# A scan kernel's outer product by TensorE for one block in eight, evictions moved to ScalarE, and the last output moved into the next stage

## The chip, the cores and the metric

One NeuronCore of a Trainium2 chip runs the whole program. The metric is the device time of one execution in microseconds (us). The profile names the engines PE (TensorE matmuls), PEld (TensorE weight loads), DVE (VectorE), ACT (ScalarE), POOL (GpSimd) and SP (SyncE, which here only issues DMAs).

## What is computed

The input has 4 images of 32 x 32 positions and 256 channels; an image is 1024 tokens. Layer 0 is a convolution block with a selective scan: layer norm, a projection to 512 channels, a depthwise 3 x 3 convolution, GELU, and then for each of 64 states a recurrence over the tokens. Layer 1 is an attention that is linear in the tokens, and a mixture of 16 experts of which each token takes two. Cut to what matters:

```python
proj = x @ w_x;  dt_raw, Bm, Cm = split(proj)           # 16, 64 and 64 columns
dt = softplus(dt_raw @ w_dt + dt_bias);  A = -exp(A_log)
def step(h, inp):                                       # over the 1024 tokens
    dA = exp(dtt[:, :, None] * A)
    h = dA * h + (dtt * xt)[:, :, None] * Bt[:, None, :]
    return h, einsum('bdn,bn->bd', h, Ct)
y = layernorm(ys + x * D_skip) * g2 + b2
x = src + y @ w_out + b_out                             # end of layer 0
t = x as tokens
t = t + attention(ln(t));  t = t + experts(ln(t))       # layer 1
```

## The kernel before, in words

**The scan.** The work is cut into 8 units: 4 images times two halves of 512 tokens. Unit 2b is the first half of image b, unit 2b+1 the second half, which starts from the state that the first half left (`last`, line 714). A unit runs over 64 states n, and each state over 4 blocks m of 128 channels: 256 slots a unit, one scan instruction a slot. In a slot:

- `scale` (line 684, ACT): `bx`, the 512 channels of 128 tokens (block j) times B of those tokens, tokens on the partitions. Four of them make a state.
- `decay` (line 692, ACT): `da`, exp(dt * A) for one block of channels.
- `turn` (line 698, PE): four 128 x 128 transposes bring `bx` into a PSUM bank with channels on the partitions; three banks rotate.
- `scan` (line 704, DVE): the recurrence over 512 tokens. After the fourth block POOL multiplies the whole state by C (line 719), from `cb_n`, which SP fetches three states ahead.
- `add_up` (line 726, PE): four transposes add the product into the four banks of y, 9 slots later.

The order of the scan's instructions is written out by hand (`manual_schedule`, lines 803 to 864): at slot k the program issues `scale(k+8)`, `decay(k+4)`, `scan(k)`, `turn(k+3)`, `add_up(k-9)`. Each engine runs its own instructions in that order. `da` has 6 buffers and `bx` 12.

**The planner.** Work of neighbouring units is laid into the slots beside the scan (`beside`, line 753). It comes as lists of pieces (gap, engine, cost, what): `head` (layer norm and input projection, 16 long matmuls), `conv` (36 taps of the 3 x 3 convolution, line 378), `dt_bc` (dt, B and C of the next unit), `after_stats` and `after` (layer norm, output projection and residual of the unit before). Each list has a window of slots, over which its pieces fall due evenly (`CONV1 = (16, 170)` and so on, lines 793 to 798). In a slot an engine takes at most about 1.0 us of such work, by the planner's costs. The pieces that use PE share one PSUM bank, `bg`: a list takes it, runs on without regard to its due times until an eviction frees it, and then the next list may take it, in a later slot. In `conv` a group of 9 taps stands 2 slots apart, so its 36 taps cover 72 of the 256 slots. Evictions from `bg` are `put_pad` (344), `put` of conv (392), `put_dtx` (534), `put` of after (610), all on DVE.

**The last unit's output.** After the last slot, lines 866 to 871 run `after_stats`, `roots_after` and `after` for unit 7 with nothing beside them. It is written to `td` in DRAM.

**Attention.** Line 925 on: loads of the weights, loads of all four images from `td` (line 941), then the preparation of the weights (lines 945 to 1004: means taken out of the columns, and the value and output matrices multiplied), then a loop over the 4 images (line 1018): statistics (1011), `xh` (1023), transposes (120), `pqk` (1037), `pv` (1054), `pkv` (1089), `po` (1134), the gate (1161). The order of this part is set by the tile framework's own scheduler, not by hand. Routing and the experts follow from line 1210.

Of the kernel before, what the change touches and what calls it, by code (L numbers as in the profile page):

```python
# [16 lines left out]
P = 128  # L17
# [16 lines left out]
def conv_ssm_attn_moe_kernel(ctx: ExitStack, tc: tile.TileContext, a: dict, out: bass.AP):  # L34
# [92 lines left out]
    def blk(i, n=BANK):  # L127
        return slice(i * n, (i + 1) * n)
# [5 lines left out]

    with ExitStack() as l0:
# [3 lines left out]
        scanp = l0.enter_context(tc.tile_pool(name="scan", bufs=2))  # L139
        ps_y = l0.enter_context(tc.tile_pool(name="ps_y", bufs=1, space=PSUM))  # L140
        ps_w = l0.enter_context(tc.tile_pool(name="ps_w", bufs=3, space=PSUM))
# [38 lines left out]
        w_o = load_rows("L0_conv_w_out", DK, C, w0)  # L180
        b_o = load_bcast("L0_conv_b_out", C, w0)
# [33 lines left out]
        for m in range(DK):  # L215
            pad = w0.tile([P, HH + 2, WW + 2], F32, name=f"pad{m}")
            nc.gpsimd.memset(pad, 0.0)
            pads.append(pad)

        def late_weights():  # L220
# [9 lines left out]
            for m in range(DK):  # L230
                nc.vector.tensor_scalar(
                    diag_d[:, m, :], ident, dsk[:, m : m + 1], None, ALU.mult
                )

# [64 lines left out]
        def head(b, g, lo=0, hi=TPB):  # L299
# [26 lines left out]
            for i in range(lo, hi):  # L326
# [6 lines left out]
                todo.append(piece(2, "DVE", 0.42, lambda i=i: put(i), "free"))  # L333
# [9 lines left out]
            def put_pad(m):  # L343
                nc.vector.tensor_scalar(
                    pads[m][:, 1 + g * ROWS + lo * RPT : 1 + g * ROWS + hi * RPT, 1 : 1 + WW],
                    made["bg"][:, : (hi - lo) * P].rearrange("p (h w) -> p h w", w=WW),
                    b_in[:, m : m + 1], None, ALU.add,
                )

            for m in range(DK):  # L350
# [4 lines left out]
                todo.append(piece(3, "DVE", 0.75, lambda m=m: put_pad(m), "free"))  # L355
            return todo

        def conv(v):
# [30 lines left out]
            def put(m):  # L389
                if m == 0:  # L390
                    made["xg", v] = acts.tile([P, DK, BANK], F32, name="xg")
                nc.vector.tensor_scalar(
                    made["xg", v][:, m, :], made["bg"], cb[:, m : m + 1], None, ALU.add
                )
# [8 lines left out]
            for m in range(DK):  # L403
# [8 lines left out]
                todo.append(piece(3, "DVE", 0.69, lambda m=m: put(m), "free"))  # L412
# [3 lines left out]
        def dt_bc(w, needs):  # L416
# [22 lines left out]
            def put_bc():  # L439
# [3 lines left out]
                nc.sync.dma_start(out=cd, in_=t[NS:, :])  # L443
                made["bct"], made["cd", w] = t, cd
# [88 lines left out]
            def put_dtx(m):  # L533
                nc.vector.tensor_copy(  # L534
# [28 lines left out]
            for m in range(DK):  # L563
                todo.append(piece(4 if m == 0 else 1, "PE", 0.44, lambda m=m: turn_dtx(m), "take"))
                todo.append(piece(
                    2, "DVE", 0.69,
# [20 lines left out]
        def after(u, need):  # L587
# [20 lines left out]
            def put(j):  # L608
                t = pre.tile([P, DK, P], F32, name="yT")
                nc.vector.tensor_copy(t, made["bg"].rearrange("p (m t) -> p m t", m=DK))  # L610
# [19 lines left out]
            for j in range(TPB):  # L630
# [5 lines left out]
                todo.append(piece(2, "DVE", 0.69, lambda j=j: put(j), "free"))  # L636
# [7 lines left out]
            return parts + [todo]  # L644

# [37 lines left out]

        def scale(s, j):
            u, n = steps[s]
            t = scanp.tile([P, DN], F32, name="bx", bufs=12)
# [790 lines left out]
```

## Time and profile before

| | us |
|---|---|
| median of 3 runs | 3609.48 (3608.98 to 3614.11) |
| the profiled execution | 3609.15 |
| its span, first to last instruction | 3607.3 |
| before the first scan instruction | 129.7 |
| units 0 to 7 of the scan | 330.0, 341.3, 335.3, 341.3, 335.6, 337.3, 328.1, 317.9 |
| end of the last scan instruction | 2796.5 |
| first attention transpose (line 120) | 2842.1 |
| start of routing (line 1225) | 3095.1 |

The units are counted from the first scan instruction (line 712) of one to that of the next. Between the execution's time and its span lie 1.85 us. A unit's length divided by 256 is the mean time of a slot, about 1.31 us. In the groups of instructions a mean duration is longer than the distance between two starts, because neighbours overlap by some 0.1 us: what an engine can do in a unit is counted by the distance from start to start in a stretch without idle time, which the timeline shows.

### The profile page before, as it was taken

To read this page: it belongs to the slowest core of one execution; us is meant where nothing else is said; L and a number is where in the kernel's file an instruction comes from. 1 tells how busy PE (TensorE), PEld (TensorE's weight loads), DVE (VectorE), ACT (ScalarE), POOL (GpSimd) and SP (SyncE) were. 2 spreads that over 40 slices of the span, in tenths; PEclk is the share of its full clock that TensorE was granted. 3 is DMA by queue.
4 is the path that set the end of the run, shared out by engine and by line. 5 is a ranking of instruction groups with operands and counts; after the bars stand their busy time and mean duration, and the time that the engine had idled before them with its cause. 6 is when DMAs were issued, how large, how long until landed. Compare 5 with 4: busy or idle time off the path is not lost.

```text
span 3607.3 us, 60573 instructions
## 1 busy us (share of the span) xinstructions
PE 3245.6 (90%) x22292; PEld 2626.9 (73%) x22292; DVE 2981.9 (83%) x3398; ACT 2863.8 (79%) x4748; POOL 2484.2 (69%) x906
## 2 busy tenths in 40 slices
PE   8989999999998998999999989898999788599995
PEld 3678777777777777777777777777777455399985
DVE  5799999999999999999999999999999666622224
ACT  1799999999999999999999999999999244121211
POOL 0489878987897798879878987998888110033331
PEclk9999999999999999999999999999999999699997
DMA  3223222212222122222222122222121200299996
GB/s 101 64 55 76 56 64 65 61 57 58 71 69 60 62 62 61 64 63 66 60 64 64 57 59 54 55 58 57 55 60 55 73 24 12 100 381 325 319 302 236
DMA packets 355165, 334.41 MB, mean 93 GB/s; under 512 B 162081, under 2 KB 241441, under 8 KB 354866
## 3 DMA queue, kind: packets, MB, share of 16 engines
q1 hardware_dynamic: 334834, 306.21, 29.1%
q0 software_dynamic: 7104, 19.41, 1.6%
q10 hardware_dynamic: 12928, 4.89, 0.5%
q8 instruction: 177, 2.90, 0.3%
q14 instruction: 122, 1.00, 0.1%
HBM read 304.21 MB, written 25.69 MB: 91 GB/s over the span
## 4 chain that ended last, share of the span: by engine, by line
ACT 60%; PE 20%; DMA 8%; DVE 7%; issue 2%; POOL 0%; POOLq 0%; DVEq 0%; ACTq 0%; SPq 0%
ACT da L695 28%; ACT bx L687 28%; DMA yd<-yb,dst 6%; PE ps L701 4%; PE y L733 3%; PE p L1377 3%; DVE h L712 3%; PE pqk L1037 2%; PE bg L382 1%; PE pf L1389 1%; DMA xb<-xd,src 1%; PE pv L1054 1%; PE ps L382 1%; PE ps_t L120 1%; ACT L695 1%
## 5 line engine op out<-in xcount | busy, mean ns | idle before, releaser
L719 POOL TENSOR_TENSOR h<-h,cb_n 128x2048 f32<-128x2048 f32 x512 | 2143.6, 4192 | 416.7 <-DVE h L712 328.0
L701 PE MATMUL ps<-ident,bx 128*128 128x128 f32 x8192 | 1323.3, 283 | 197.8 <-DVE h L712 138.0
L687 ACT ACTIVATE bx<-dtxT,bT 128x512 f32<-128x512 f32 x2048 | 1451.5, 709 | 16.5 <-DVE dtxT L534 16.5
L695 ACT ACTIVATE da<-dt,l_conv_a_log_sb 128x512 f32<-128x512 f32 x2048 | 1452.2, 709 | 13.6 <-DVE h L712 13.3
L701 PEld LDWEIGHTS ps<-ident,bx 128*128 128x128 f32 x8192 | 937.2, 142 | 632.8 <-DVE h L712 307.9
L712 DVE TENSOR_TENSOR_SCAN h<-da,last,ps 128x512 f32<-128x512 f32 x1024 | 1231.6, 1263 | 30.3 <-ACT da L695 21.6
L733 PE MATMUL y<-ident,h 128*128 128x128 f32 x8192 | 1246.1, 275 | 5.7 <-POOL h L719 5.6
L712 DVE TENSOR_TENSOR_SCAN h<-da,ps 128x512 f32<-128x512 f32 x1024 | 1189.5, 1207 | 49.4 <-ACT da L695 32.6
L733 PEld LDWEIGHTS y<-ident,h 128*128 128x128 f32 x8192 | 974.5, 143 | 7.8 <-POOL h L719 6.7
L1383 DVE TENSOR_TENSOR hT<-s,p 128x256 f32<-128x256 f32 x148 | 62.4, 421 | 336.4 <-ACT s L1382 336.4
L1377 PE MATMUL p<-xT,w 128*128 128x128 f32 x2368 | 291.6, 277 | 0.5 <-ACT xT L1366 0.5
L1377 PEld LDWEIGHTS p<-xT,w 128*128 128x128 f32 x2368 | 285.1, 194 | 4.8 <-ACT xT L1366 0.9
L1382 ACT ACTIVATE s<-p 128x256 f32<-128x256 f32 x148 | 56.9, 384 | 275.5 <-PE p L1377 275.5
L1397 POOL DMA_INDIRECT yd<-yb,dst x74 | 73.2, 990 | 264.5 <-DMA yd<-yb,dst 185.9
L382 PE MATMUL bg<-pad,dgc 128*128 128x512 f32 x432 | 222.2, 596 | 0.0
L1346 POOL DMA_INDIRECT xb<-xd,src x74 | 72.1, 975 | 132.8 <-DVE dst L1318 108.7
L1389 PE MATMUL pf<-w,hT 128*128 128x256 f32 x592 | 153.3, 382 | 0.1
L1051 POOL TENSOR_TENSOR t_all<-t_all,bcat 128x256 f32<-128x256 f32 x32 | 23.0, 747 | 164.6 <-ACT xh L1023 159.9
L1389 PEld LDWEIGHTS pf<-w,hT 128*128 128x128 f32 x592 | 101.7, 192 | 8.2 <-DVE hT L1383 0.5
L1366 ACT COPY xT<-px 128x256 f32<-128x256 f32 x74 | 27.6, 372 | 77.5 <-PE px L1364 77.5
L382 PEld LDWEIGHTS bg<-pad,dgc 128*128 128x128 f32 x432 | 65.5, 192 | 0.0
L382 PE MATMUL ps<-pad,dgc 128*128 128x512 f32 x144 | 64.0, 605 | 0.7 <-DVE e L487 0.7
(287 smaller groups left out, 2056.5 us busy)
## 6 DMA issues: line engine op xcount, KB each, us to landing
cb_n<-cd SPq DMA_DIRECT2D x512, 256.0 KB, 3.3
w<-in_L_ffn_w_dram SPq DMA_DIRECT2D x222, 512.0 KB, 6.2
dgc<-diags SPq DMA_DIRECT2D x84, 192.0 KB, 3.1
y<-yd SPq DMA_DIRECT2D x8, 1024.0 KB, 9.6
last<-h SPq DMA_DIRECT2D x256, 2.0 KB, 2.9
xr<-in_x_dram SPq DMA_DIRECT2D x32, 128.0 KB, 3.2
td<-xr SPq DMA_DIRECT2D x32, 128.0 KB, 3.3
t_all<-td SPq DMA_DIRECT2D x4, 1024.0 KB, 10.0
```

Source lines behind the costliest of these rows:

```text
L382: nc.tensor.matmul(made["bg"].rearrange("p (h w) -> p h w", w=WW), made["dgc", m * 3 + i][:, j, :], pads[m][:, half * ROWS + i : (half + 1 ...
L687: nc.scalar.activation(t, made["dtxT", u][:, j, :], AF.Copy, scale=made["bT", u][:, j, n : n + 1])
L695: nc.scalar.activation(t, made["dt", u][:, m, :], AF.Exp, scale=A[:, m, n : n + 1])
L701: nc.tensor.transpose(t[:, blk(j, P)], made["bx", s, j][:, blk(m, P)], ident)
L712: nc.vector.tensor_tensor_scan(h[:, m, 1:], made.pop(("da", s, m)), made.pop(("dbx", s, m)), 0.0 if seg == 0 else last[b][:, n, m : m + 1] ...
L719: nc.gpsimd.tensor_tensor(h[:, :, :BANK], h[:, :, 1:], over_middle(made["c", s], DK), ALU.mult)
L733: nc.tensor.matmul(made["y", u][j][:, blk(m, P)], made["h", s][:, m, blk(j, P)], ident, is_transpose=True, start=n == 0 and m == 0, stop=n ...
L1037: nc.tensor.matmul(pqk.rearrange("p s c -> p (s c)"), xhT[:, ck, blk(i, P)], wcat[:, ck, : 2 * C], start=(ck == 0), stop=(ck == CK - 1),)
L1346: nc.gpsimd.indirect_dma_start(t, None, xd[:, :], bass.IndirectOffsetOnAxis(src[:, i : i + 1], 0))
L1377: nc.tensor.matmul(p12[:, j, s, :], on[w, i][:, ck, blk(h + j, P)], on["xT", i][:, ck, :], start=(ck == 0), stop=(ck == CK - 1),)
L1389: nc.tensor.matmul(on["pf", i], on["hT", i][:, hk, :], on["w3", i][:, hk, :], start=(hk == 0), stop=(hk == HK - 1),)
L1397: nc.gpsimd.indirect_dma_start(yd[:, :], bass.IndirectOffsetOnAxis(dst[:, i : i + 1], 0), yb, None)
```

## The change

1. **B on a diagonal.** In units 1 to 7, for even states n and the first block of tokens (j = 0), `scale` issues nothing. In its place `turn` multiplies: the block of `dtxT` (128 tokens by 128 channels) is the stationary operand and a 128 x 128 matrix with B on its diagonal the moving one, so that the product is already turned. The other three blocks stay as they were. The matrices lie in DRAM (32 for each of two units in turn): they are set to zero once, in unit 0 (slots 4 and 14), `put_bc` of each later unit writes the diagonals with a DMA of single elements, and `fetch_diagonal` loads a 64 KB matrix three states ahead, on SP's queue, into one of 3 buffers. `bx` goes from 12 buffers to 11.
2. **Evictions on ScalarE.** While an odd unit is scanned, `put_pad`, `put` of conv, `put_dtx` and `put` of after run on ACT; while an even one is, `put` of after alone. The planner's windows are new.
3. **Attention's weights** are prepared by a planner's list, `matrices`, beside unit 6, in the memory of the convolution's padded images. Their evictions run on DVE.
4. **The last half.** The output of unit 7 is no longer computed after the scan. Its sum `ysb`, `w_o` and `b_o` are kept, the residual is loaded straight from x into `t_all`, and `last_half` computes it in attention, ahead of the second image. `t_all`'s loads no longer wait for a write of unit 7. The two PSUM pools of layer 0 are opened in the other order.

```diff
+        ps_w = l0.enter_context(tc.tile_pool(name="ps_w", bufs=3, space=PSUM))
         ps_y = l0.enter_context(tc.tile_pool(name="ps_y", bufs=1, space=PSUM))
-        ps_w = l0.enter_context(tc.tile_pool(name="ps_w", bufs=3, space=PSUM))
...
+        diag_b = [dram.tile([NS // 2, P, P], F32, name=f"diag_b{k}") for k in range(2)]
+        zero = scanp.tile([P, P], F32, name="zero", tag="dgb", bufs=3)
+        nc.vector.memset(zero, 0.0)
+        def zero_diagonals(k):
+            nc.sync.dma_start(
+                out=diag_b[k].rearrange("n a b -> a n b"), in_=over_middle(zero, NS // 2)
+            )
...
+                if on_scalar("pad"):
+                    nc.scalar.activation(pad, bg, AF.Identity, bias=b_in[:, m : m + 1])
+                else:
+                    nc.vector.tensor_scalar(pad, bg, b_in[:, m : m + 1], None, ALU.add)
...
+                if on_scalar("xg"):
+                    nc.scalar.activation(xg, made["bg"], AF.Identity, bias=cb[:, m : m + 1])
+                else:
+                    nc.vector.tensor_scalar(xg, made["bg"], cb[:, m : m + 1], None, ALU.add)
...
                 nc.sync.dma_start(out=cd, in_=t[NS:, :])
+                if w > 0:
+                    with nc.allow_non_contiguous_dma(reason="diagonals"):
+                        nc.sync.dma_start(
+                            out=diag_b[w % 2].rearrange("n a b -> n (a b)")[:, :: P + 1],
+                            in_=t[:NS:2, :P],
+                        )
...
             def put_dtx(m):
-                nc.vector.tensor_copy(
+                (nc.scalar.copy if on_scalar("dtx") else nc.vector.tensor_copy)(
...
+                (nc.scalar.copy if on_scalar("yT") else nc.vector.tensor_copy)(
+                    t, made["bg"].rearrange("p (m t) -> p m t", m=DK)
+                )
...
+        def on_scalar(what):
+            return not alone and what in (ODD if made["u"] % 2 else EVEN)
...
+        def by_diagonal(s, j):
+            u, n = steps[s]
+            return j == 0 and (n % 2 == 0) and u > 0
+        def fetch_diagonal(s):
+            u, n = steps[s]
+            t = scanp.tile([P, P], F32, name="dgb", bufs=3)
+            nc.sync.dma_start(out=t, in_=diag_b[u % 2][n // 2])
+            made["dgb", s] = t
         def scale(s, j):
             u, n = steps[s]
-            t = scanp.tile([P, DN], F32, name="bx", bufs=12)
+            if by_diagonal(s, j):
+                return
+            t = scanp.tile([P, DN], F32, name="bx", bufs=11)
...
-                nc.tensor.transpose(t[:, blk(j, P)], made["bx", s, j][:, blk(m, P)], ident)
+                if by_diagonal(s, j):
+                    nc.tensor.matmul(
+                        t[:, blk(j, P)], made["dtxT", steps[s][0]][:, j, blk(m, P)],
+                        made["dgb", s], start=True, stop=True,
+                    )
+                else:
+                    nc.tensor.transpose(t[:, blk(j, P)], made["bx", s, j][:, blk(m, P)], ident)
...
+            if v == n:
+                lists.append([(matrices(), MATS)])
...
-        SKIP = (11, 27)
-        HEAD1, CONV0 = (11, 50), (50, 236)
-        CONV1, HEAD0 = (16, 170), (176, 240)
-        STATS = (11, 60)
-        DT = ((11, 35), (35, 84), (86, 90), (92, 190), (192, 240))
-        AFTER = ((14, 110), (112, 245))
+        ODD, EVEN = ("pad", "xg", "yT", "dtx", ), ("yT", )
+        SKIP = (11, 24)
+        HEAD1, CONV0 = (14, 85), (50, 236)
+        CONV1, HEAD0 = (22, 176), (200, 240)
+        STATS = (11, 69)
+        DT = ((11, 38), (51, 64), (81, 93), (94, 184), (185, 240))
+        AFTER = ((36, 132), (139, 229))
+        MATS = (44, 245)
...
+                if k in (4, 14):
+                    zero_diagonals(1 if k == 4 else 0)
                 if at % DK == 1 and k > DK and k // DK + 3 < len(steps):
                     fetch(k // DK + 3)
+                    if by_diagonal(k // DK + 3, 0):
+                        fetch_diagonal(k // DK + 3)
...
-        alone = True
-        u = len(units) - 1
-        run(after_stats(u))
-        logs(made["rs"], made["mv"][:, :, 1])
-        roots_after(u)
-        run(*after(u, None))
...
+        for b in range(NB - 1):
+            nc.sync.dma_start(out=tbs[b], in_=rows(td, b))
+        nc.sync.dma_start(out=tbs[-1][:, :TPB, :], in_=rows(td, NB - 1)[:, :TPB, :])
+        nc.sync.dma_start(out=tbs[-1][:, TPB:, :], in_=rows(xf, NB - 1)[:, TPB:, :])
...
+        def last_half():
+            ysb = made["ysb", len(units) - 1]
+            _, rs = statistics(ysb, "ln1", TPB)
+            for j in range(TPB):
+                t = tbs[-1][:, TPB + j, :]
+                nc.gpsimd.tensor_tensor(t, t, b_o, ALU.add)
+                ps = ps_b.tile([P, BANK], F32, name="ps_l", tag="po")
+                for m in range(DK):
+                    nc.tensor.transpose(ps[:, blk(m, P)], ysb[:, j, blk(m, P)], ident)
+                yT = sm.tile([P, BANK], F32, name="yT")
+                nc.vector.tensor_copy(yT, ps)
+                po = ps_b.tile([P, C], F32, name="po_l", tag="po")
+                for m in range(DK):
+                    nc.tensor.matmul(
+                        po, yT[:, blk(m, P)], w_o[:, m, :], start=(m == 0), stop=(m == DK - 1)
+                    )
+                nc.vector.scalar_tensor_tensor(
+                    t, po, rs[:, j : j + 1], t, ALU.mult, ALU.add
+                )
         for b in range(NB):
+            if b == 1:
+                last_half()
...
```

## The prediction

> **What bounds the kernel now.** First the chain of work that ended last, by engine:
>
> ```profile
> ACT 60%; PE 20%; DMA 8%; DVE 7%; issue 2%; POOL 0%; POOLq 0%; DVEq 0%; ACTq 0%; SPq 0%
> ```
>
> ACT carries 60% of the span, in two lines (da, bx). Then busy time in stretches, cut at the units (here 1, 2, 6 and 7; columns: length, then busy PE, PEld, DVE, ACT, POOL, granted clock):
>
> ```profile
> 459.70:801.00 341.30, 315.32 (x2276) 258.93 (x2276) 329.34 (x302) 335.09 (x537) 290.75 (x89) 0.98 0.21 62
> 801.00:1136.30 335.30, 311.35 (x2278) 257.13 (x2277) 318.76 (x303) 329.54 (x529) 290.57 (x89) 0.99 0.27 64
> ...
> 2150.50:2478.60 328.10, 298.76 (x2173) 240.35 (x2172) 314.78 (x290) 326.00 (x526) 290.56 (x89) 0.98 0.24 56
> 2478.60:2796.50 317.90, 290.08 (x2131) 230.93 (x2132) 314.47 (x274) 314.31 (x512) 273.03 (x75) 1.00 0.19 56
> ```
>
> ACT is busy 98 to 99% of every unit; DVE is 3 to 11 us behind it. Then the timelines, for the pace of each engine. ACT, one start to the next 0.613 us; DVE in an odd unit, 35.23/30 = 1.17 us (1.11 in an even one: unit 0's first turns, each released by a scan, start at 138.70, 139.81, 140.92, 142.03):
>
> ```profile
> 2342.28 0.71 ACT L687 ACTIVATE bx<-dtxT,bT 128x512 f32<-128x512 f32 x1
> 2342.90 0.71 ACT L695 ACTIVATE da<-dt,l_conv_a_log_sb 128x512 f32<-128x512 f32 x1
> ```
>
> ```profile
> 2544.85 35.23 DVE L712 TENSOR_TENSOR_SCAN h<-da,last,ps 128x512 f32<-128x512 f32 x30
> ```
>
> A slot so takes ACT 2 x 0.613 = 1.226 us and DVE 1.11 or 1.17. PE, in a group of convolution taps:
>
> ```profile
> 355.44 1.02 PE L382 MATMUL bg<-pad,dgc 128*128 128x512 f32 x2
> 356.31 0.60 PE L701 MATMUL ps<-ident,bx 128*128 128x128 f32 x4
> 356.74 0.60 PE L733 MATMUL y<-ident,h 128*128 128x128 f32 x4
> 357.18 0.60 PE L701 MATMUL ps<-ident,bx 128*128 128x128 f32 x4
> 357.62 0.60 PE L733 MATMUL y<-ident,h 128*128 128x128 f32 x4
> 358.05 1.02 PE L382 MATMUL bg<-pad,dgc 128*128 128x512 f32 x2
> ```
>
> From tap to tap 2.61 us without a gap for two slots: **PE, not ACT, sets the pace in the 72 tap slots** (1.304 against ACT's 1.226). Four transposes take 0.437, a slot's eight 0.874.
>
> This makes a model of a unit: tap slots 72 x 1.304 = 93.9; the other 184 at ACT's 1.226 = 225.6; and ACT's remaining work (table loads, exp, ln, GELU), its busy time less 256 x 1.226 = 313.9. Unit 1: 93.9 + 225.6 + 21.2 = 340.7 (measured 341.3); unit 2: 15.6, 335.1 (335.3); unit 5 (busy 331.1): 17.2, 336.7 (337.3). It holds to 0.7 us.
>
> **The diagonal.** ACT loses 32 instructions a unit, 32 x 0.613 = 19.6 us, over 7 units 137. PE: the matmul isn't in the trace with these operands, but the skip product (line 741) has its form, 128 x 128 by a diagonal:
>
> ```profile
> 486.88 0.39 PE L741 MATMUL y<-diag_d,xg 128*128 128x128 f32 x2
> 487.10 0.60 PE L701 MATMUL ps<-ident,bx 128*128 128x128 f32 x4
> 487.54 0.60 PE L733 MATMUL y<-ident,h 128*128 128x128 f32 x4
> ```
>
> A product is two instructions, 0.22 us, a transpose one, 0.109. Four of them a state: 4 x (0.224 - 0.109) = 0.46 us, 14.7 a unit; a tap slot goes to 1.304 + 0.46/8 = 1.361 on average.
>
> The Trainium skill ("TensorE: Matmul & The Clock Gate", Terms) speaks against the change: it calls the transpose mode "4× faster for FP32". By that a product would cost 0.436 and a unit 32 x 4 x 0.327 = 42 us of PE; its rows here, two instructions of the same pace against one, make it 2, and the row decides. With 42 instead of 14.7, a tap slot would be 1.468, 105.7 a unit.
>
> DMAs: a 64 KB fetch every second state, behind a cb_n fetch of 256 KB that lands in 3.3 us and is issued three states (some 15 us) ahead: hidden, and without that cover 3 us for each. The scatter is 4096 elements; packets of 4 bytes take 9 ns in the trace, over 16 engines 2.3 us. The zeroing, 2 x 4096 packets of 512 bytes, nearest row 576 bytes at 29 ns: 7.4 us each, in front of fetches with some 12 us to spare. SP's issue: 0.61 us for 512 elements (line 724), so about 5 for 4096 pro rata, beside the same 12. All at nothing; at worst 15 us once.
>
> **Evictions.** Counted from the lists: pad 2 x 4, xg and dtx 3 x 4 each, yT 7 x 4, 60 in all: 16 in units 1 and 3, 12 in unit 5, 4 in 2, 4, 6 and 7. On DVE pad and xg start 0.64 us apart from their successor, yT and dtx 0.58. On ACT a PSUM copy of this size (line 750, 474.19 to 475.13 for two) takes 0.47; with a bias from memory no row shows it: between 0.47 and the 0.613 of bx, which has a scale from memory; I take the middle, 0.54. Unit 1: ACT 8 x 0.47 + 8 x 0.54 = +8.1, DVE 8 x 0.64 + 8 x 0.58 = -9.8. Unit 5: +5.9 and -7.2. An even unit: +1.9 and -2.3.
>
> **Units after.** Tap slots 72 x 1.361 = 98.0. Others at ACT's 1.226 - 0.613/8 = 1.149: 211.5. ACT's rest in unit 1 21.2 + 8.1 = 29.3; sum 338.8, plus the 0.6 the model lacked: 339.4, **a gain of 1.9 only**, since all of ACT's rest stands outside the taps. Even (17.5): 327.2, gain 8.1. Unit 5 (23.1): 333.3, gain 4.0. But in tap slots ACT now has 0.21 us to spare a slot, 3.8 a group, and may run ahead as far as `da`'s two spare buffers let it. That a lead exists the run of 30 scans shows: DVE went 30 x 0.055 = 1.7 us faster than ACT without waiting. I take 2 us for each of 4 groups: 8 less. Unit 1: 331.4. Unit 2: ACT 319.2; but DVE, 98.0 + 184 x 1.111 + its own rest 23.8 - 2.3 = 323.9, is later: 323.9. (23.8, start to start: dt 4 x 1.33, statistics 4 x 0.80, evictions 9.8, xT 4 x 0.32, xr 4 x 0.38, ysb 1.2, three small copies 1.5; unit 5 has no head, 3.8 less, unit 6 no convolution either.) Unit 5: ACT 325.3; DVE 98.0 + 184 x 1.171 + 20.0 - 7.2 = 326.3: 326.3. Gains: units 1 and 3 9.9 each, 2 and 4 11.5 each, 5 11.0: 53.8.
>
> Unit 6 has no taps: ACT 326.0 - 19.6 + 1.9 = 308.3; DVE 256 x 1.111 + 17.0 - 2.3 + 8.3 = 307.4, where 8.3 is `matrices` (14 evictions and sums of the rows at lines 958 to 1003, 0.3 to 0.7 each). Two engines level lose more to each other than the 2.1 us now lost: 5; 313, gain 15. Unit 7: DVE 299.8 + 7.9 - 2.3 = 305.4 and the 4 now lost: 309.4, gain 8.5. Unit 0: nothing. **Scan: 77 us** (without the lead: 1.9 x 2 + 8.1 x 2 + 4.0 + 12 + 6 = 42).
>
> **The end of the scan.**
>
> ```profile
> 2800.87 1.96 PE L733 MATMUL y<-ident,h 128*128 128x128 f32 x16 [2.71 <-POOL h L719]
> ...
> 2826.86 5.64 SPq L941 DMA_DIRECT2D t_all<-td  x4
> ...
> 2842.12 3.94 PE L120 MATMUL ps_t<-ident,xh 128*128 128x128 f32 x12 [5.95 <-ACT xh L1023]
> ```
>
> The last scan ends at 2796.5, y's last product starts at 2800.87 and is evicted from 2802.5; then 24 us go to unit 7's output and the loads, and only at 2842.1 (45.6 after the scan) does attention transpose. The first image's statistics start at 2834.9, 8.0 after the loads' issue (shortest landing 7.8). After: loads issued when y is done (6.0 after the scan), 0.3 + 7.8 to land, then the 7.2 from statistics to transposes: 21.3, gain 24. If the memory comes free with the last `da`, earlier, DVE's ysb copies (7.2 after the scan) come last: 14.4, gain 31. `last_half`: PE 4 x (4 x 0.109 + 8 x 0.216) = 8.7, DVE 7.8. In an image's 61.7 us PE is busy 53.9, so some of it fits into gaps: between 0 and 8.7, I take 5. **Net 19** (15 to 31).
>
> **Sum.** 77 + 19 = 96. The profiled execution's span 3607.3 - 96 = 3511; with the 1.85 around it 3513; the median of the runs is 0.3 above that execution: 3513.
>
> **Rivals.** *No lead*: ACT's rest stays wholly outside the taps, PE the bound inside: 42 + 15 = 57, 3552. For it: the old tap slots left ACT 0.08 us each, and no lead is seen in the model. *All hidden*: each unit as long as its busiest engine: 323.6 (units 1, 3), 311.8 (2, 4), 317.4, 308.3, 305.4, gain 135, with 31: 3443; the new windows would have to spread everything evenly; half-way from the forecast is 3478. *Slower*: an eviction on ACT stands behind ACT's backlog, and PE's next `bg` matmul waits for it with turns and add-ups queued behind, which DVE needs. ACT issues `da` four slots ahead of use, so where it is late its slot k comes up to 3 slots, 3.7 us, after DVE's: 60 evictions at 2.5 make 3513 + 150 = 3663; from 1.6 us each the kernel is slower. Against it: while PE waits ACT doesn't, so it catches up, and ACT's own sum has fallen. *It does nothing*: the matrices come late and their wait replaces the products saved: 3590 to 3620.
>
> **Chances.** Forecast (3490 to 3535) 0.53, no lead 0.20, towards all hidden 0.16, slower 0.08, nothing 0.03. The range of 8 in 10 takes in the forecast, most of the hidden case and no lead: 3465 to 3558. What a measurement of this kernel can tell from no change is about 0.2%, 7 us: faster 0.89, same 0.03, slower 0.08.
>
> **What will show it.** Right: units 1 to 5 at 324 to 332; ACT below 98% busy and DVE as busy; product instructions 0.11 apart; taps 2.6 to 2.9 us apart; the first transpose some 21 us after the scan. Wrong: PE or DVE idle for ACT's evictions, units over 338, half-clock stretches (granted clock below 0.97 in the units), POOL or PE idle for a DMA, attention's images longer than 66.

## The result, and the profile after

The changed kernel takes 3557.13 us in the median of 4 runs (3549.48 to 3564.42); the kernel before took 3611.8 beside it. The ratio is 0.9838, 95% interval 0.9821 to 0.9854. The direction is the forecast one and the time lies at the end of the range (3558): 55 us were gained where 96 were forecast, almost what the rival *No lead* gave (57). It is not that rival's sum, as the parts show. They are of the profiled executions, whose spans are 3607.3 and 3562.6:

| part | gain forecast | gain measured |
|---|---|---|
| units 1 to 5 | 53.8 | 35.6 |
| unit 6 | 15 | -4.7 |
| units 0 and 7 | 0 and 8.5 | 0.2 and 10.7 |
| last scan to first transpose of attention | 24 | 29.6 |
| attention, with `last_half` | -5 | -13.0 |
| before the scan | 0 | -4.8 |
| from routing on | 0 | -8.9 |
| sum | 96 | 44.7 |

The two stretches at the ends vary with the execution: over the 13 kernels profiled here, all with the same experts and nearly the same start, the time before the scan lies between 129.7 and 134.7 us and that from routing on between 509.9 and 521.1. Attention with `last_half`, the same in 11 of them, takes 263.0 to 269.3. The profiled execution of the changed kernel (3564.42 us) was the slowest of its four, so its sum falls 10 short of the medians' 54.7. Scan units whose work is the same in several kernels agree within 0.5 us in nearly all cases, so the experiments are read by units.

The chain of work that ended last, by engine, in the kernel after. ACT falls from 60% to 42%, and PE rises from 20% to 37%:

```profile
ACT 42%; PE 37%; DVE 9%; DMA 6%; issue 2%; POOL 0%; DVEq 0%; POOLq 0%; ACTq 0%; SPq 0%
```

Busy time in units 1, 2, 6 and 7 of the kernel after (columns as before):

```profile
464.30:798.00 333.70, 321.71 (x2403) 272.40 (x2402) 319.67 (x286) 322.92 (x518) 290.32 (x90) 1.00 0.24 70
798.00:1126.80 328.80, 319.93 (x2408) 274.39 (x2407) 311.82 (x298) 315.75 (x504) 290.47 (x89) 0.99 0.30 72
...
2119.50:2452.30 332.80, 305.93 (x2326) 265.48 (x2324) 322.78 (x304) 314.34 (x504) 291.78 (x90) 0.98 0.28 66
2452.30:2759.50 307.20, 294.67 (x2260) 252.40 (x2259) 306.05 (x271) 295.24 (x479) 271.72 (x74) 0.99 0.21 64
```

In units 1 and 2 three engines are busy 95 to 97% of the time, and none of them the whole of it. Unit 7 runs at DVE's pace, 306 of 307 us. Unit 6 got longer than before, and DVE's busy time in it rose by 8 us to 323.

The chain within unit 2, by line, before and after:

```profile
by line: ACT da L695 37.1%; ACT bx L687 37.0%; PE ps L701 5.3%; PE y L733 4.8%; DVE h L712 3.8%; PE bg L382 2.3%; PE bg L338 1.5%; issue 1.4%; ACT L695 0.8%; PE bg L476 0.6%; ACT s L511 0.6%; ACT e L493 0.6%; ACT dtxT L498 0.6%; ACT xg L398
```

```profile
by line: PE y L914 25.0%; PE ps L882 23.3%; PE bg L404 9.4%; ACT da L870 8.2%; PE ps L877 7.7%; ACT bx L862 7.1%; DVE h L893 4.8%; PE bg L650 1.6%; issue 1.5%; PE bg L508 1.3%; PE bg L449 1.2%; PE y L922 1.1%; PE bg L460 1.1%; ACT L870 0.8%
```

Before, 74% of the unit are ScalarE's `da` and `bx`. After, `y`, `ps` and `bg` of TensorE hold some 70%: far more than the 72 of 256 slots with convolution taps, in which the forecast had let TensorE set the pace. Unit 4 is like it. In the odd units it is otherwise; unit 1 after:

```profile
by line: ACT da L870 30.5%; ACT bx L862 26.9%; PE y L914 8.7%; PE ps L882 8.0%; DVE h L893 4.9%; PE ps L877 3.3%; PE bg L404 2.3%; PE bg L357 1.6%; issue 1.3%; PE bg L449 1.2%; PE bg L460 1.0%; PE y L922 1.0%; ACT L870 0.8%; ACT xg L416 0.7
```

ScalarE's `da` and `bx` still hold 57% there and in unit 3, and 62% in unit 5, after 70% in unit 1 before; TensorE has about the taps' share. Where engines are nearly level, such a chain is no proof: in unit 7 it runs 75% through `da` and `bx`, while ScalarE was busy 295 us of 307 and DVE 306.

### The profile page after: what moved, and what is told of

It reads as the page before. It is cut to its first block, busy times and chain, and to the rows that moved or that the text cites. A ratio compares the mean times of both kernels' runs of the same rounds, so it can differ in the third digit from the quotient of the medians.

```text
span 3562.6 us, 62683 instructions
## 1 busy us (share of the span) xinstructions
PE 3292.8 (92%) x23188; PEld 2744.0 (77%) x23188; DVE 2933.6 (82%) x3342; ACT 2764.9 (78%) x4577; POOL 2481.9 (70%) x901
## 4 chain that ended last, share of the span: by engine, by line
ACT 42%; PE 37%; DVE 9%; DMA 6%; issue 2%; POOL 0%; DVEq 0%; POOLq 0%; ACTq 0%; SPq 0%
ACT da L870 20%; ACT bx L862 18%; PE y L914 8%; PE ps L882 8%; DVE h L893 4%; PE p L1519 4%; DMA yd<-yb,dst 4%; PE ps L877 3%; PE bg L404 2%; DMA xb<-xd,src 2%; PE pf L1531 2%; PE pqk L1179 2%; PE pv L1196 1%; PE ps L404 1%; PE ps_t L120 1%
## 5 line engine op out<-in xcount | busy, mean ns | idle before, releaser
L862 ACT ACTIVATE bx<-dtxT,bT 128x512 f32<-128x512 f32 x1824 | 1308.0, 717 | 17.7 <-DVE dtxT L566 17.7
L882 PE MATMUL ps<-ident,bx 128*128 128x128 f32 x7296 | 1171.6, 278 | 74.2 <-DVE h L893 51.7
L893 DVE TENSOR_TENSOR_SCAN h<-da,ps 128x512 f32<-128x512 f32 x1024 | 1170.7, 1201 | 43.1 <-ACT da L870 19.4
L882 PEld LDWEIGHTS ps<-ident,bx 128*128 128x128 f32 x7296 | 854.2, 142 | 299.9 <-DVE h L893 144.9
L877 PE MATMUL ps<-dgb,dtxT 128*128 128x128 f32 x1792 | 387.5, 298 | 31.1 <-DVE h L893 21.9
L877 PEld LDWEIGHTS ps<-dgb,dtxT 128*128 128x128 f32 x1792 | 281.3, 190 | 168.4 <-DVE h L893 88.6
L1193 POOL TENSOR_TENSOR t_all<-t_all,brow 128x256 f32<-128x256 f32 x32 | 23.2, 747 | 179.7 <-ACT xh L1165 179.7
L1508 ACT COPY xT<-px 128x256 f32<-128x256 f32 x74 | 27.5, 372 | 83.1 <-PE px L1506 83.1
```

The source lines that it names most:

```text
L862: nc.scalar.activation(t, made["dtxT", u][:, j, :], AF.Copy, scale=made["bT", u][:, j, n : n + 1])
L877: nc.tensor.matmul(t[:, blk(j, P)], made["dtxT", steps[s][0]][:, j, blk(m, P)], made["dgb", s], start=True, stop=True,)
L882: nc.tensor.transpose(t[:, blk(j, P)], made["bx", s, j][:, blk(m, P)], ident)
L893: nc.vector.tensor_tensor_scan(h[:, m, 1:], made.pop(("da", s, m)), made.pop(("dbx", s, m)), 0.0 if seg == 0 else last[b][:, n, m : m + 1] ...
```

## The experiments

Theory at the outset: the shortfall has two places. In unit 6 DVE's instructions on the rows of the weights stand still while POOL works (rival: unit 6 is a matter of the windows). In units 1 to 5 ScalarE's lead is cut short by its buffers (rival: TensorE's extra work, or the unevenness of the work along the unit). Lengths of the units in all profiles:

| kernel | 0 | 1 | 2 | 3 | 4 | 5 | 6 | 7 | scan |
|---|---|---|---|---|---|---|---|---|---|
| before | 330.0 | 341.3 | 335.3 | 341.3 | 335.6 | 337.3 | 328.1 | 317.9 | 2666.9 |
| after | 329.8 | 333.7 | 328.8 | 333.7 | 328.8 | 330.2 | 332.8 | 307.2 | 2625.1 |
| no_diag | 330.4 | 344.0 | 335.8 | 343.9 | 336.4 | 340.2 | 341.6 | 320.4 | 2692.8 |
| diag_only | 329.4 | 340.2 | 336.0 | 339.9 | 335.9 | 336.0 | 318.8 | 309.5 | 2645.7 |
| no_evict | 329.8 | 336.4 | 330.4 | 336.4 | 330.3 | 332.5 | 336.0 | 309.5 | 2641.4 |
| free_block | 329.8 | 330.7 | 323.3 | 330.7 | 323.6 | 327.0 | 330.8 | 307.0 | 2602.9 |
| rows_act | 329.8 | 333.8 | 328.8 | 333.8 | 328.8 | 330.1 | 323.6 | 307.2 | 2615.8 |
| rows_one | 329.8 | 333.9 | 328.7 | 333.8 | 328.6 | 330.1 | 336.9 | 307.2 | 2628.9 |
| da8 | 329.8 | 333.8 | 328.8 | 333.7 | 328.7 | 330.2 | 323.4 | 307.2 | 2615.6 |
| spread | 329.9 | 336.1 | 329.1 | 336.0 | 328.7 | 332.6 | 324.9 | 307.2 | 2624.4 |
| moved | 338.3 | 330.0 | 328.4 | 329.7 | 328.7 | 327.4 | 323.2 | 307.2 | 2612.8 |
| place | 337.2 | 330.8 | 329.1 | 330.5 | 329.2 | 327.2 | 329.5 | 307.2 | 2620.6 |
| spread_zero | 329.8 | 329.6 | 328.7 | 329.3 | 330.9 | 327.4 | 323.1 | 307.1 | 2606.1 |

### Unit 6: rows_act and rows_one

DVE's timeline in unit 6 of the kernel after, and POOL's beside it:

```profile
2299.40 6.74 DVE L893 TENSOR_TENSOR_SCAN h<-da,ps 128x512 f32<-128x512 f32 x6
2306.07 4.36 DVE L729 SCALAR_TENSOR_TENSOR wqk<-w_mean,wqk 128x256 f32<-128x256 f32 x1
2310.35 4.54 DVE L893 TENSOR_TENSOR_SCAN h<-da,ps 128x512 f32<-128x512 f32 x4
```

```profile
2305.94 4.20 POOL L900 TENSOR_TENSOR h<-h,cb_n 128x2048 f32<-128x2048 f32 x1
2310.08 1.48 POOL L554 TENSOR_TENSOR dt<-dt,e 128x512 f32<-128x512 f32 x1
```

The subtraction on 256 elements takes 4.36 us: it starts 0.13 us after POOL's product with C and ends 0.3 us after it. All six of line 729 end 0.28 us after the end of such a product, wherever in it they started; the shortest of the four on wqk took 0.56. In the kernel before, without a product beside it, this subtraction took 0.42. The six took 14.5 us together; the forecast had put 0.3 to 0.7 each. rows_act does them on ScalarE:

```diff
-                nc.vector.scalar_tensor_tensor(
-                    w[:, blk(s, C)], m[:, s : s + 1].to_broadcast([P, C]), -1.0 / C,
-                    w[:, blk(s, C)], ALU.mult, ALU.add,
+                if s == 0:
+                    nc.scalar.activation(m, m, AF.Copy, scale=-1.0 / C)
+                nc.scalar.activation(
+                    w[:, blk(s, C)], w[:, blk(s, C)], AF.Identity, bias=m[:, s : s + 1]
```

> The changed kernel, but the six subtractions of row means in the preparation of attention's weights (L729), whose two inputs both lie in SBUF, run on ACT with the mean as a bias in place of DVE. Theory: on DVE they stood still until POOL's multiply had ended (0.56 to 4.36 us each where 0.42 is their length), 12 us in all, and with what that delayed they cost unit 6 its 15 to 20 us: unit 6 goes from 332.8 to 313 to 318 us, the median from 3557 to about 3541. Rival: the stalls have another cause (the weights' loads, PE's half clock after the gap): unit 6 stays at 330 to 335 and the median at 3557, or some 3 us above it.

Measured: 3543.94 us (3541.45 to 3548.15), ratio 0.9805 (0.9778 to 0.9832). Unit 6 goes from 332.8 to 323.6, every other unit stays. So 9.2 us of unit 6 are these six instructions; the expected 313 to 318 was not reached.

rows_one keeps them on DVE, with one operand of this size in SBUF in place of two:

```diff
-                nc.scalar.activation(
-                    w[:, blk(s, C)], w[:, blk(s, C)], AF.Identity, bias=m[:, s : s + 1]
+                nc.vector.tensor_scalar(
+                    w[:, blk(s, C)], w[:, blk(s, C)], m[:, s : s + 1], None, ALU.add
```

> rows_act with the six subtractions in the rows of w_qk and w_brow back on DVE, but in a form with one operand of 128x512 in SBUF (tensor_scalar with a column per partition) in place of the two of scalar_tensor_tensor; the mean column is scaled by ScalarE. Theory two operands: it is two reads from SBUF that stand still while POOL's product runs; then the six take 0.3-0.5 us each and unit 6 stays at 322-325. Rival: any fp32 instruction of DVE from SBUF to SBUF stands still behind POOL (the copy of bvw, one operand, took 1.09 us in unit 6 where 0.30 was usual); then the six take 1 to 4 us each and unit 6 is at 329-334.

Measured: one run, 3554.47 us; unit 6 takes 336.9. The rival holds for the six instructions, which take 1.7 to 4.3 us each and all end 0.15 us after a product of POOL; the unit is 3 us past the rival's 329 to 334, and DVE waited 2.8 us in it for the scaled column. DVE's groups in unit 6 of rows_one (mean ns after the busy us):

```profile
L731 DVE TENSOR_SCALAR wqk<-wqk,w_mean 128x256 f32<-128x256 f32 x4 | 12.2, 3054 | 2.8 <-ACT w_mean L730 2.8
L731 DVE TENSOR_SCALAR brow<-brow,b_mean 128x256 f32<-128x256 f32 x2 | 4.7, 2366 | 0.0
L745 DVE COPY wvs<-bg 128x512 f32<-128x512 f32 x2 | 1.3, 668 | 0.0
L721 DVE SCALAR_TENSOR_TENSOR wqk<-bg,wqk 128x512 f32<-128x512 f32 x2 | 1.3, 664 | 0.0
L726 DVE TENSOR_REDUCE w_mean<-wqk 128x2 f32<-128x512 f32 x2 | 1.3, 662 | 0.0
```

The instruction with one operand is held as long as that with two. Twice its size from PSUM (`bg`) takes 0.66, and so does the sum over a row in SBUF. What counts is thus the form and not the amount. The Trainium skill has a rule that the prediction should have weighed against its 0.3 to 0.7: "GPSIMD Engine Reference" (Specifications) gives GpSimd's SBUF interfaces as shared with VectorE, in contention with instructions that have two SBUF inputs or run in a two-port mode, and "VectorE: DVE Perf Modes" (Mode 2×_2P) says that fp32 `tensor_scalar` from SBUF to SBUF is in that mode. Both halves agree with the rows: 2.38 us a piece for the one form, 3.05 and 2.37 for the other, 0.66 for those that are neither.

### The parts of the change alone: no_diag, diag_only, no_evict

no_diag turns the diagonal off and keeps the windows, the evictions, the weights and the tail:

```diff
-            return j == 0 and (n % 2 == 0) and u > 0
+            return False
```

> The changed kernel without the diagonal: all blocks of bx by ACT and turned by transposes, no matrices, no zeroing; evictions on ACT, windows, weights beside unit 6 and the last half in attention stay. Theory: ACT's 19.6 us a unit come back on top of 8.1 us of evictions, so ACT is the bound: units 1 and 3 at 344 to 348, 2 and 4 at 333 to 337, unit 7 at 316 to 320, together some 45 us over the changed kernel, median 3600. Rival: the diagonal gains nothing since PE gives back what ACT saves: units within 3 us of 333.7 and 328.8, median 3557.

Measured: 3624.1 us, ratio 1.0024 (1.0008 to 1.0041). The theory holds in units 1 to 4 within 0.1 us; the rival falls. Beside the new windows the diagonal is worth 67.7 us of the scan. Without it all the rest is a small loss: the scan is 26 us longer than before (half of it in unit 6), and the tail takes 16 of it back (29.6 less 13.5).

diag_only puts the diagonal alone into the kernel before: `by_diagonal`, the matrices and their DMAs as in the diff, nothing else but `bx` at 11 buffers.

> The kernel before with the diagonal alone: old windows, evictions on DVE, last output where it was. The model of the prediction (72 tap slots at 1.361 us, 184 at 1.149, ScalarE's rest) gives 339.4 for unit 1 without a lead and 331 with one, and 333.3 for unit 5. Theory: the diagonal is worth about 67 us in the new kernel (run no_diag), of which a part needs the evictions' move to ScalarE; alone it gives odd units 336-339, even 328-331, unit 6 312-316 (it has no rows of w_qk there), unit 7 308-311, the tail unchanged, the median 3565-3580. Rival: DVE, which keeps its evictions (busy 329 of 341 us before), becomes the bound at once; odd units 339-341, even 332-335, median over 3590.

Measured: 3594.94 us (3589.28 to 3598.5), ratio 0.9942 (0.992 to 0.9964). Neither expectation holds as a whole. Units 6 and 7 get shorter by 9.3 and 8.4, but units 1 to 5 get 1.1, -0.7, 1.4, -0.3 and 1.3: next to nothing. So the parts do not add up: the scan gains 21 by the one, loses 26 by the other, and gains 42 by both. In units 1 to 5 the diagonal pays only with the new windows. Its chain in unit 2 of diag_only:

```profile
by line: PE y L767 22.8%; PE ps L735 20.9%; PE bg L391 9.5%; ACT da L723 8.3%; ACT bx L715 7.1%; PE ps L730 6.7%; DVE h L746 6.4%; issue 2.5%; PE bg L347 2.0%; PE bg L491 1.3%; POOL h L753 1.2%; PE bg L432 1.1%; PE y L775 1.1%; PE bg L443 1
```

ScalarE's `da` and `bx` hold 15% here, from 74% before, and TensorE two thirds: as far as the chain shows it, TensorE took ScalarE's place at once.

no_evict is the changed kernel with all evictions on DVE:

```diff
-        ODD, EVEN = ("pad", "xg", "yT", "dtx", ), ("yT", )
+        ODD, EVEN = (), ()
```

> The changed kernel with every eviction back on DVE (both lists of names empty); the diagonal, the windows and the rest stay. Theory: DVE gets 9.8 us more in units 1 and 3 and is the bound there: 336 to 340 in place of 333.7, even units 329 to 331, unit 7 309.5; median 3557 + 10 to 20. Rival: evictions on ACT delay PE's next matmul on the one shared bank and cost more than DVE's relief gives: units 1, 3 and 5 below 331, median 3545.

Measured: 3572.62 us, ratio 0.9886 (0.9855 to 0.9916). The theory holds. The evictions' move is worth 16 us of the scan, 1.5 to 3.2 in each of units 1 to 7. Between diag_only and no_evict units 1 to 5 differ in the windows (and in the order in which two PSUM pools are opened), and these are worth 3.5 to 5.6 each, 22 together. The forecast had no term for the windows.

### TensorE's extra work: free_block

free_block leaves out the product of the first block for every second state and turns the block next to it in its place, by plain transposes; the matrices aren't fetched.

```diff
-                if by_diagonal(s, j):
-                    nc.tensor.matmul(
...
-                else:
-                    nc.tensor.transpose(t[:, blk(j, P)], made["bx", s, j][:, blk(m, P)], ident)
+                i = 1 if by_diagonal(s, j) else j
+                nc.tensor.transpose(t[:, blk(j, P)], made["bx", s, i][:, blk(m, P)], ident)
```

> The changed kernel with the diagonal's product left out: block 0 of every second state is taken from block 1's bx by plain transposes, so that neither ACT nor PE works for it and no matrix is fetched (this leaves B's product for these blocks out). It shows what PE's 14.7 us a unit cost. Theory: PE sets the pace of the 72 tap slots, 4.1 us a unit there, and the even units that came out 5 us above the forecast are PE's too: units 1 to 5 4 to 8 us shorter (326 to 330, 321 to 325), units 6 and 7 within 2 us, median about 3530. Rival: ACT's and DVE's own work outside the taps is the bound: all units within 2 us, median 3552 to 3560.

Measured: 3533.46 us, ratio 0.9777 (0.9748 to 0.9806). TensorE's share of the price is 3.0 us in odd units, 5.5 and 5.2 in units 2 and 4, 3.2 in unit 5, and some 2 in unit 6 where no taps are. The forecast had 4.1 a unit, in the taps. This term was sized well: 4.0 in the mean of units 1 to 5, although the odd units stay below the 4 to 8 of the theory. Its place was right too. Taps of unit 1 in the kernel after, the first two with a product in each of the slots between them, the last two with none:

```profile
520.34 1.02 PE L404 MATMUL bg<-pad,dgc 128*128 128x512 f32 x2
...
523.18 1.02 PE L404 MATMUL bg<-pad,dgc 128*128 128x512 f32 x2
...
525.78 1.02 PE L404 MATMUL bg<-pad,dgc 128*128 128x512 f32 x2
```

2.84 and 2.60 us; in the mean over the groups 2.72, which is the forecast's 2 x 1.361. What the taps cost is thus as forecast, and what units 1 to 5 took beyond the forecast lies in the other 184 slots. Two sizes of a product are seen in the kernel after, in a row without gaps and after a wait of TensorE:

```profile
690.81 0.39 PE L877 MATMUL ps<-dgb,dtxT 128*128 128x128 f32 x2
691.03 0.49 PE L882 MATMUL ps<-ident,bx 128*128 128x128 f32 x3
...
862.13 0.46 PE L877 MATMUL ps<-dgb,dtxT 128*128 128x128 f32 x2 [0.28 <-DVE h L893]
862.43 0.49 PE L882 MATMUL ps<-ident,bx 128*128 128x128 f32 x3
```

0.22 us, as forecast, in 480 of 896 cases; about 0.3 in 407 others, nearly all of which started late after the instruction before them, so that TensorE had waited. Whether the 0.08 us more cost time isn't shown.

### ScalarE's lead: da8

ScalarE's waits in units 1 to 5 of rows_act (us in all, times, longest) begin with `da`, for a buffer that a scan still reads:

```profile
ACT da L871 <- DVE h L894: 28.4, 45, 2.5
ACT e L525 <- DVE e L519: 18.0, 10, 2.0
```

```diff
-            t = scanp.tile([P, BANK], F32, name="da", bufs=6)
+            t = scanp.tile([P, BANK], F32, name="da", bufs=8)
```

(and two `dgb` buffers in place of three, for the room)

> rows_act with eight da buffers in place of six (and two dgb in place of three, for the room). Lead theory: in the changed kernel's scan ScalarE's da waits 28.5 us for a buffer that DVE's scan still holds (45 times), although ScalarE has time to spare in the tap slots; with two more buffers ScalarE runs further ahead there and its rest no longer stands outside the taps. Then the odd units go from 333.8 to 328-331, the even ones from 328.8 to 324-327, the scan from 2615.8 to 2590-2602, the median to some 3518-3532. Rival: the three engines are level and DVE, whose busy time is 320 of 334 us, sets the pace whatever the lead; units 1 to 5 within 1 us of rows_act, median 3540-3548.

Measured: 3546.35 us (3544.14 to 3547.1), ratio 0.9809 (0.979 to 0.9827); all units within 0.2 of rows_act: the rival holds. The wait for `da` is gone, and the same time is waited elsewhere:

```profile
ACT e L525 <- DVE e L519: 20.3, 10, 2.9
ACT bx L863 <- PE ps L883: 15.2, 19, 1.6
ACT yT L642 <- PE bg L636: 14.4, 6, 3.1
ACT xg L416 <- PE bg L404: 9.5, 3, 3.2
ACT da L871 <- DVE h L894: 1.8, 5, 0.8
```

The lead theory falls. ScalarE waits because the other two are behind it; running further ahead brings none of them forward: DVE waits 27.6 us for `ps` and 14.8 for `da`, after 27.5 and 14.6 in rows_act. Some of ScalarE's wait is now for `bx`, whose 11 buffers no run increases.

### The unevenness along the unit: spread, moved, place, spread_zero

For every instruction the distance to the next start on its engine was taken, at the lower quartile of its group, so that waits drop out, and summed per engine over stretches of the unit. For unit 2:

```
             ACT    DVE    PE     sum of the longest, by stretches of 8 slots    measured
before       328.5  307.9  288.4  334.4                                          335.3
diag_only    307.0  307.9  302.6  329.4                                          336.0
after        312.6  305.5  302.9  327.1                                          328.8
```

Over the whole unit the busiest engine has 307.9 us of work in diag_only, and the unit takes 336.0. The sum of the longest engine by stretches of 8 slots comes nearer, and in the kernel after very near (333.0 of 333.7 in unit 1). In the kernel before ScalarE was the longest in 20 of 32 stretches; in the kernel after it is in 16, and DVE and TensorE in 8 each. A reckoning by unit sums can't see this.

That the sum comes near is no proof by itself. It is taken from the times at which the work was done, so it can hardly pass the unit's length, and shorter stretches bring it nearer whatever the cause. If the stretches are cut instead where each engine reaches a slot in its own order of instructions, unit 2 of the kernel after gives 337.0 by 8 slots, 328.3 by 16 and 323.2 by 32 (by 16, diag_only gives 331.5 of its 336.0): which length is the right one was not measured. What tests the idea is to move work.

spread puts the small matmuls of dt, B and C further apart, two slots in place of one:

```diff
-                    4 if m == 0 else 1, "PE", 0.86, lambda m=m: low(m), "" if m else "take",
+                    4 if m == 0 else 2, "PE", 0.86, lambda m=m: low(m), "" if m else "take",
...
-                todo.append(piece(1, "PE", 0.86, lambda m=m: bc(m), "" if m else "take"))
+                todo.append(piece(1 if m == 0 else 2, "PE", 0.86, lambda m=m: bc(m), "" if m else "take"))
```

> rows_act with the small matmuls of dt, B and C (low and bc) two slots apart in place of one. Theory burst: part of what units 1 to 3 lose against their busiest engine is lost where PE has several of these in successive slots; then units 1 to 3 are 1 to 4 us shorter each, the median 3533-3541. Rival: the loss is spread over the unit and the windows' ends are what counts; units within 1 us or longer by up to 3, median 3542-3552.

Measured: 3554.93 us (3553.29 to 3558.14), ratio 0.9835 (0.9815 to 0.9854): slower than rows_act, the odd units by some 2.3, as the rival allowed. That these bursts cost something is not borne out.

moved leaves the sums of the engines alone and moves the 32 products of a unit, by hand, to the stretches in which ScalarE was the longest:

```diff
-            return j == 0 and (n % 2 == 0) and u > 0
+            return j == 0 and AT[u][n] == "1"
```

> rows_act with the same 32 products by diagonal a unit, but laid by hand to other states in units 1 to 6: out of the stretches in which TensorE's work is the longest of the three engines, into those in which ScalarE's is (matrices for all 64 states in DRAM, five buffers in place of three). The engines' sums over a unit do not change. Theory stretches: a unit lasts as long as the sum, over stretches of some 8 slots, of the longest engine's work in each; by that sum units 1 to 6 get shorter by 4.3, 2.5, 4.1, 2.7, 4.0 and 3.4, in all 21, and with half of it lost again the scan goes from 2615.8 to some 2595-2606, the median 3523-3536. Rival: ScalarE's lead of a few slots already evens this out, or DVE bounds; units within 1 us, median 3540-3548.

Measured: 3543.8 us (3542.92 to 3546.72), ratio 0.9811 (0.9786 to 0.9836). Odd units get shorter by 3.8, 4.1 and 2.7, near what the stretches said (4.3, 4.1, 4.0); units 2, 4 and 6 by 0.1 to 0.4 where 2.5 to 3.4 were expected. In all 11.5 of 21. Work of the same amount in other places is thus worth 3 to 4 us in an odd unit: the unevenness is shown there, and in the even units it isn't. The two more buffers are not the reason: in rows_act TensorE waits 0.6 us in all for matrices. Taken again from moved's own trace, the sums by 8 slots fall by 2.8, 3.6 and 3.1 in the odd units and by 0.3 at most in the even ones, so what failed in these was the forecast of what the move does to the sum; why stays open. Unit 0 took most of the gain back, 8.5 us longer. There the zeroings are 4 MB each now, and behind one, on SyncE's queue, stands the copy of a state's last column:

```profile
155.58 0.43 SPq L248 DMA_DIRECT2D diag_b<-zero  x1
156.12 15.70 SPq L917 DMA_DIRECT2D last<-h  x1
```

```profile
174.37 3.44 DVE L905 TENSOR_TENSOR_SCAN h<-da,ps 128x512 f32<-128x512 f32 x3 [7.29 <-DMA last<-h]
```

The copy took 15.7 us to issue, and DVE waited 7.3 for the `h` buffer that it reads.

place, with the number of products free too:

> As moved, but the number of products is free as well: 41, 36, 41, 37, 42 and 52 in units 1 to 6, wherever ScalarE's work is the longest of a stretch. Theory stretches: units 1 to 6 get shorter by 5.3, 2.5, 5.3, 2.8, 5.1 and 7.0, in all 28; with half of it lost again the scan goes to 2588-2602, the median 3515-3532. Rival: TensorE becomes the longest in more stretches than the sum knows of, or the added matrices' DMAs come late; units as in rows_act or longer, median over 3540.

Measured: 3553.74 us (3547.71 to 3557.27), ratio 0.9832 (0.9805 to 0.9859). More products bring nothing beyond moved's in units 1, 3 and 5 and cost 6 in unit 6. The theory falls; the rival holds for the even units and the median, while units 1, 3 and 5 stay 3 below rows_act. In unit 6 TensorE waits 5.6 us for matrices (1.4 in moved), and POOL 6.3 for `cb_n` where it waited 3.1 in moved.

spread_zero cuts moved's two zeroings into four of 2 MB:

```diff
-                if k in (4, 14):
-                    zero_diagonals(1 if k == 4 else 0)
+                if k in (4, 14, 64, 96):
+                    zero_diagonals(1 if k < 64 else 0, 0 if k in (4, 64) else 1)
```

> moved, with its two zeroings of 4 MB cut into four of 2 MB, the size of the changed kernel's, at slots 4, 14, 64 and 96. In the run moved unit 0 was 8.5 us longer than in rows_act, and DVE waited 8.5 us (7.3 of it once) for loads of the kept state that stood behind a zeroing on SyncE's queue. Theory queue: with 2 MB at a time unit 0 is back at 329.8, units 1 to 6 stay as in moved (330.0, 328.4, 329.7, 328.7, 327.4, 323.2), the scan is 2604-2605, the median 3529-3537, below every other kernel of this study. Rival: it is the bytes in all, not the length of one transfer, that delays the loads; unit 0 stays at 335 or more, the median 3538-3545.

Measured: 3535.54 us (3529.18 to 3541.35), ratio 0.9777 (0.9761 to 0.9793). Unit 0 is back at 329.8 and DVE's wait for the copy is gone, with as many bytes in all: the length of one transfer was the cause. It is not the second zeroing coming close behind the first: behind moved's first one, too, the next issue took 10.1 us, and 3.5 here. Unit 4 took 2.2 us more than in moved, all of it in one stretch of 16 slots with the same work; why stays open. This is the fastest complete kernel of the study by its median, 21.6 us below the changed one; against rows_act the intervals overlap, and only the scan, 9.7 shorter in the profiles, tells them apart.

## Why the prediction was right, and where it was wrong

**Right: what bounds the kernel, and the sign.** ScalarE was the bound: with 224 of its instructions taken away (137 us by the forecast's price) its share of the chain fell from 60% to 42%, and the other two came level with it. As forecast, ScalarE fell below 98% busy and DVE is nearly as busy, and the units 1 to 5, forecast at 331.4, 323.9, 331.4, 323.9 and 326.3, came out 2.3 to 4.9 longer: units 1 and 3 above the 324 to 332 named as right, all below the 338 named as wrong. The rival *Slower* is refuted: TensorE's waits in units 1 to 5 for an eviction on ScalarE come to some 6 us in all. From rows_act, whose units 1 to 5 are those of the kernel after:

```profile
PE bg L330 <- ACT dtxT L566: 2.5, 2, 1.2
PE bg L404 <- ACT yT L642: 1.9, 3, 0.6
PE bg L330 <- ACT yT L642: 1.2, 2, 0.6
```

**Right: the product and the DMAs.** Two instructions 0.11 us apart against one; free_block found 3.0 to 5.5 us in each of units 1 to 5 where the forecast had 4.1, and the taps stand 2.72 us apart. The factor of 4 that the Trainium skill states ("TensorE: Matmul & The Clock Gate", Terms) would have made 42 us of TensorE's time a unit, by the prediction's estimate; the measurement decides for 2. The zeroings of 2 MB, the scatter and the fetches cost nothing (unit 0: 329.8 against 330.0). The scatter took 0.61 us to issue, where the forecast had reckoned about 5 pro rata. The forecast's 12 us of cover was not far from its edge: twice the length cost 8.5 us in moved.

**Wrong: "8.3 is `matrices` (... 0.3 to 0.7 each)".** This is the largest single miss, 19.7 us in unit 6. Six of the fourteen took 14.5 us. rows_act gives 9.2 back. The other 10.5 (323.6 against 313) no run takes apart; by stretches of 8 slots the longest engines sum to 321.3 there, 9 above ScalarE's own 312.4. The rows from which 0.3 to 0.7 was taken were of attention's start, where POOL does not multiply states.

**Wrong: "I take 2 us for each of 4 groups".** The lead was to carry ScalarE's spare time in the tap slots over to its rest. da8 shows that two more buffers of lead are worth nothing; what the two spare ones of the kernel gave, no run shows. The step before it failed with it in the even units: that in the 184 slots without taps ScalarE or DVE alone sets the pace and TensorE has room. The taps took what was forecast, yet units 2 and 4 came out 4.9 longer, free_block takes 5.5 and 5.2 off them, and TensorE holds 70% of their chain. In the odd units ScalarE still holds 57% or more, and there moved shows that the place of the same work along the unit is worth 3 to 4 us: the engines take turns at being the longest. Units 1 to 5 gained 35.6, between *No lead* (24) and the forecast (53.8).

**Missing: the windows.** The forecast gave them no price, and with the diagonal they are worth 22 us of units 1 to 5 (diag_only against no_evict). Without them the forecast's own sum for an even unit without a lead, 8.1 us of gain, was 0.7 of loss (unit 2 of diag_only, whose evictions are still on DVE). That the time came out near *No lead*, and within the range at all, is so luck in part, a sum of misses: the diagonal was worth less in units 1 to 5 than that rival said, the windows more, and unit 6 and the tail went their own ways.

**The tail.** The memory came free with the last `da`: the loads are issued as the last scan ends, and the first transposes follow 16.0 us later. The forecast named this case, 14.4 and a gain of 31, and took the other (21.3 and 24). The chain of the kernel after:

```profile
2757.14 2.46 DVE h L893 x2
2759.61 8.23 DMA t_all<-td
...
2768.29 0.75 DVE ln_st L1130 x2
...
2775.53 4.00 PE ps_t L120 x12
```

`last_half` cost the whole of its TensorE work and more, and the image that it delays passed the 66 us that the forecast had named as a sign of being wrong. The second image in the kernel before and after:

```profile
2907.40:2968.54 61.14, 54.01 (x211) 34.83 (x209) 42.30 (x108) 25.18 (x61) 5.81 (x8) 0.92 0.05 18
```

```profile
2841.85:2912.75 70.90, 62.89 (x254) 41.85 (x253) 47.92 (x125) 25.31 (x62) 5.80 (x8) 0.93 0.05 16
```

TensorE is busy 8.9 us more, and the image is 9.8 longer: nothing of it fell into gaps, although 7 us of them were there. The forecast's 5 was too little, and its bound of 8.7 was passed. Net, the two are 16.6 with all of attention, against 19; attention alone varies by some 6 us from kernel to kernel.

## What to carry to other kernels

When a change takes work off the one engine that bounds a stretch, look at how its work and that of the others lies along it, in pieces of some slots, before and after: three engines that are level over a unit and uneven within it can lose more than any of their sums shows, and here two more buffers did not even this out. Do not take the duration of an instruction of DVE from a place where POOL rests, if it is to run where POOL works; look at its operands, and put elementwise SBUF-to-SBUF work beside a busy POOL on ScalarE. A transfer that costs nothing may cost much at twice its length, if a short one stands behind it on the same queue: cut it.

## What the runs showed of the hardware

- A DVE instruction on 128 x 256 fp32 from SBUF to SBUF took up to 4.36 us beside POOL's 4.2 us product, and 0.56 at best; in `tensor_scalar`'s form up to 4.32. Each ended just after the product did, 0.28 us in the first form and 0.15 in the second. Row sums in SBUF (0.66) and all forms with a PSUM operand (0.40 for 256 elements, 0.66 for 512) were not held up.
- A 4 MB DMA of 512-byte pieces made the next DMA on its queue take 10.1 and 15.7 us to issue (moved); behind 2 MB it took 3.7 and 6.6, and the scan lost nothing (the kernel after).
- ScalarE did the same subtraction in 0.50 us, beside POOL.
